# Attention scores on 32-by-32 tiles of TensorE in place of 32-by-128 ones

## The chip, the cores and the metric

The kernel runs on one core of one Trainium2 chip. The metric is the device time of one execution in microseconds (us). Before the change it is 2890.68 us, the median of three runs (2889.41 to 2895.76).

## The reference, cut to what matters

The input x is an image of 256 x 256 positions with 128 channels, float32. Two layers follow each other, each added to its input. The change touches only the first, an attention along rows: every one of the 256 rows `s` is an attention of its own, with 256 queries, 256 keys, 4 heads and 32 channels per head.

```python
q = split_heads(jnp.einsum('...qi,oi->...qo', q_x, wq)) / np.sqrt(C_HIDDEN)
k = split_heads(jnp.einsum('...ki,oi->...ko', kv_x, wk))
v = split_heads(jnp.einsum('...ki,oi->...ko', kv_x, wv))
a = jnp.einsum('bshqd,bshkd->bshqk', q, k)
a = a + bias1 + bias2
a = jax.nn.softmax(a, axis=-1)
o = jnp.einsum('bshqk,bshkd->bshqd', a, v)
...
o = o * g
...
return jnp.einsum('...qi,oi->...qo', o, wo) + bo
```

`q_x` is x after a group normalisation, `kv_x` an input of its own, `g` a sigmoid gate. The line that the change rewrites is the fifth, `a = einsum(q, k)`: for each row and head a 256 x 256 matrix from 32 channels. The second layer (spectral convolutions, a small attention over tokens and several normalisations) is computed by other functions and isn't touched.

## The kernel before, in words

The function `layer0` reads x once for the group statistics, turns the weights and the bias, and then calls `Rows.run`, which does the 256 attention rows. After that `layer1` does the second layer; in the profile the rows take from about 100 to about 1650 us of the span.

`Rows.run` is a software pipeline written out by hand: inside `manual_schedule` the order of the calls is the order of the instructions on TensorE (PE), ScalarE (ACT), VectorE (DVE) and GpSimd (POOL). Iteration `i` emits, in this order: `scores(i)`, `project(i + 1)`, `turn(i + 2)`, `weigh(i)`, `out(i - 3)`, `spectrum(i - 4)`, `attend(i - 1)`. On PE a row is therefore a chain of bursts:

- `scores` (L272): scores, transposed, keys on partitions. For each half `c` of 128 keys and each head `h`, one matmul takes 32 partitions of `qkT` (the head's channels) as contraction, 128 keys as the stationary columns, 256 queries as the moving ones. So it uses a 32 x 128 tile of the PE array. The four heads lie on partitions 0-31, 32-63, 64-95 and 96-127, so four such tiles stand under each other in the array. Each head writes to a PSUM bank of its own: `sc[0]` holds heads 0 and 1, `sc[1]` heads 2 and 3, each bank 2 x 256 float32 (both halves `c`).
- `project` (L246, L247, L252, L256): queries and keys, values and gate of the next row, 128 x 128 tiles.
- `turn` (L235, L236): transposes of the row after next.
- `out` (L333) and `spectrum` (L346, L348): the output projection, transposes and a small transform of earlier rows.
- `attend` (L311, L316): weighted sums and sums of the weights of the row before, on 128 x 32 tiles, four column quarters side by side.

The other engines: ScalarE computes exponentials of the scores in four pieces (`exp`, L281), two of them in place in PSUM, and evicts `qkT` (L249), gate (L260), `xnT` and `kvT` (L238, L240) and the transform (L352). VectorE multiplies heads 0 and 1 by the exponential of the bias (L294), scales the attended values (L322, L323, L324), adds (L337) and takes statistics (L351). GpSimd multiplies heads 2 and 3 (L299), adds the two key halves (L303) and adds the output bias (L327). The score tiles have one buffer each (`bufs=1`), so `scores(i + 1)` must wait until L294 and L281 have read those of row `i`; the other PSUM tiles of the rows share four buffers.

Everything is float32. In the records of the profile, each float32 matmul stands as two weight loads (PEld, LDWEIGHTS) and two MATMUL passes on PE; a transpose stands as one of each.

For comparison there is one more place in the kernel that uses 32 x 32 tiles: the helper `skip` in `layer1` (L1215), which runs, for four output tiles `ps[j]` and four row quarters `i`, a matmul from row quarter `i` to column quarter `i ^ j`. In the tile `ups<-y` of the second half of the channels it comes in two parts of 16 matmuls with 256 moving columns each.

```python
for j in range(4):
    for i in range(4):
        r, o = slice(32 * i, 32 * i + 32), slice(32 * (i ^ j), 32 * (i ^ j) + 32)
        w = blk[r, r] if len(blk.shape) == 2 else blk[r, j]
        nc.tensor.matmul(rows_of(ps[j][o, :])[:, n], w, part[r, j], start=(k == 0), stop=stop)
```

## Time and profile before

| what | value |
|---|---|
| median time of three runs | 2890.68 us |
| span of the profiled execution | 2888.9 us |
| PE busy | 2651.2 us, 92% of the span |
| PE weight loads busy | 1941.7 us, 67% |
| DVE busy | 2008.1 us, 70% |
| POOL busy | 1679.9 us, 58% |
| ACT busy | 1491.0 us, 52% |
| granted TensorE clock, mean | 0.952 of full |
| score matmuls (L272): records, mean pass | 4096, 400 ns |
| score loads (L272): records, mean | 4096, 184 ns |

How to read it: a group of the page is a line of the kernel with its engine, operation, tiles and shapes; then busy time, mean duration of one, and, after the bar, the idle time of that engine just before it with what ended most of it. "32*128 32x256" of a matmul is the tile of the array (contraction rows * stationary columns) and the moving operand (partitions x columns). A view by stretches gives the busy time of each engine between two times, with the number of instructions in brackets; the order of time lists start, duration, engine, line and operation, with equal neighbours merged ("x16"). The duration of a merged line reaches to the modelled end of its last instruction, so the distance between starts says more about pace than the duration does.

### The profile page before, as it was taken

To read this page: it belongs to the slowest core of one execution; us is meant where nothing else is said; L and a number is where in the kernel's file an instruction comes from. 1 tells how busy PE (TensorE), PEld (TensorE's weight loads), DVE (VectorE), ACT (ScalarE), POOL (GpSimd) and SP (SyncE) were. 2 spreads that over 40 slices of the span, in tenths; PEclk is the share of its full clock that TensorE was granted. 3 is DMA by queue.
4 is the path that set the end of the run, shared out by engine and by line. 5 is a ranking of instruction groups with operands and counts; after the bars stand their busy time and mean duration, and the time that the engine had idled before them with its cause. 6 is when DMAs were issued, how large, how long until landed. Compare 5 with 4: busy or idle time off the path is not lost. (4 is left out here: it accounts for less than half of the span.)

```text
span 2888.9 us, 71477 instructions
## 1 busy us (share of the span) xinstructions
PE 2651.2 (92%) x29116; PEld 1941.7 (67%) x29116; DVE 2008.1 (70%) x3263; ACT 1491.0 (52%) x2849; POOL 1679.9 (58%) x1308
## 2 busy tenths in 40 slices
PE   6799999999999999999999899999889988799654
PEld 6677777777777777777777656778665555455532
DVE  7788888888888888888888744756645545365555
ACT  0477777777777777777777622200004611365132
POOL 0399999999999999999999800200114833111211
PEclk9999999999999999999999989999989989799865
DMA  9422222222222222222222101188879984798599
GB/s 369 164 67 67 67 67 67 67 67 67 67 68 69 68 67 69 68 66 71 67 67 67 41 19 53 34 278 271 277 236 319 310 296 137 251 360 305 187 359 337
DMA packets 246705, 430.12 MB, mean 149 GB/s; under 512 B 26278, under 2 KB 174201, under 8 KB 239976
## 3 DMA queue, kind: packets, MB, share of 16 engines
q1 hardware_dynamic: 206568, 335.34, 34.8%
q0 software_dynamic: 22912, 81.80, 7.4%
q10 hardware_dynamic: 16896, 8.39, 1.0%
q8 instruction: 231, 3.78, 0.5%
q14 instruction: 98, 0.80, 0.1%
HBM read 290.17 MB, written 135.27 MB: 147 GB/s over the span
## 5 line engine op out<-in xcount | busy, mean ns | idle before, releaser
L299 POOL TENSOR_TENSOR e<-e,b1T 128x1024 f32<-128x1024 f32 x256 | 606.0, 2367 | 165.3 <-PE u L348 90.4
L303 POOL TENSOR_TENSOR es<-e 128x512 f32<-128x512 f32 x512 | 639.4, 1270 | 20.1
L281 ACT ACTIVATE sc<-sc,b2T 128x512 f32<-128x512 f32 x512 | 339.0, 662 | 364.7 <-PE sc L272 356.4
L323 DVE RECIPROCAL av<-av 128x256 f32<-128x256 f32 x256 | 452.3, 1767 | 27.2 <-DVE og L322 1.4
L281 ACT ACTIVATE e<-sc,b2T 128x512 f32<-128x512 f32 x512 | 348.7, 681 | 0.0
L294 DVE TENSOR_TENSOR e<-sc,b1T 128x1024 f32<-128x1024 f32 x256 | 311.1, 1215 | 0.0
L272 PE MATMUL sc<-qkT 32*128 32x256 f32 x4096 | 293.5, 400 | 1.3 <-DVE e L294 1.3
L311 PE MATMUL av<-e,v 128*32 128x256 f32 x4096 | 274.7, 385 | 0.5 <-POOL e L299 0.5
L1332 PE MATMUL yps<-xt,mpT 128*128 128x256 f32 x1024 | 247.7, 396 | 17.8 <-DVE yt L1342 9.3
L272 PEld LDWEIGHTS sc<-qkT 32*128 32x128 f32 x4096 | 185.2, 184 | 112.3 <-issue 97.8
L322 DVE SCALAR_TENSOR_TENSOR og<-gate,av 128x256 f32<-128x256 f32 x256 | 107.7, 421 | 190.6 <-PE av L316 190.6
L1332 PEld LDWEIGHTS yps<-xt,mpT 128*128 128x128 f32 x1024 | 195.9, 196 | 56.8 <-DVE yt L1342 14.7
L1346 POOL DMA_DIRECT2D yd<-yt x32 | 17.8, 555 | 346.1 <-DVE yt L1342 346.1
L327 POOL TENSOR_TENSOR x<-xt,bo 128x256 f32<-128x256 f32 x256 | 187.5, 733 | 0.0
L246 PE MATMUL qk<-xnT,wT_wq 128*128 128x256 f32 x512 | 179.5, 432 | 1.7 <-ACT xnT L238 1.7
L252 PEld LDWEIGHTS gv<-wT_wv,kvT 128*128 128x128 f32 x1024 | 155.0, 192 | 13.4
L316 PE MATMUL av<-es,ones 128*32 128x256 f32 x2048 | 157.5, 379 | 2.6 <-POOL es L303 2.5
L333 PE MATMUL wo<-wT_wo,og 128*128 128x128 f32 x1024 | 156.8, 276 | 2.7 <-DVE og L324 2.7
L311 PEld LDWEIGHTS av<-e,v 128*32 128x32 f32 x4096 | 106.9, 109 | 76.1 <-POOL e L299 1.0
L348 PE MATMUL u<-adft,x 128*128 128x129 f32 x1024 | 156.4, 275 | 0.0
L252 PE MATMUL gv<-wT_wv,kvT 128*128 128x128 f32 x1024 | 156.0, 275 | 0.0
L1699 ACT ACTIVATE blocks<-h2ps,col 128x512 f32<-128x512 f32 x128 | 89.0, 776 | 129.5 <-PE h2ps L1200 129.5
(546 smaller groups left out, 5294.4 us busy)
## 6 DMA issues: line engine op xcount, KB each, us to landing
xt<-x1d SPq DMA_DIRECT2D x128, 512.0 KB
xb<-in_x_dram SPq DMA_DIRECT2D x32, 1024.0 KB
xt<-in_x_dram SPq DMA_DIRECT2D x128, 256.0 KB
kt<-in_L_conv_kv_x_dram SPq DMA_DIRECT2D x128, 256.0 KB
x1d<-x SPq DMA_DIRECT2D x256, 128.0 KB
y<-yd SPq DMA_DIRECT2D x62, 512.0 KB
gs<-Gd SPq DMA_DIRECT2D x384, 64.0 KB
yd<-yt POOLq DMA_DIRECT2D x32, 512.0 KB, 6.0
```

Source lines behind the costliest of these rows:

```text
L246: nc.tensor.matmul(ps[:, 0:256], wT["wq"], xnT, start=True, stop=True)
L252: nc.tensor.matmul(ps[:, 256 + c * P : 256 + (c + 1) * P], kvT[:, c * P : (c + 1) * P], wT["wv"], start=True, stop=True,)
L272: nc.tensor.matmul(sc[h // 2][:, h % 2, c * 256 : (c + 1) * 256], qkT[p, 256 + c * P : 256 + (c + 1) * P], qkT[p, 0:256], start=True, stop ...
L281: nc.scalar.activation(r["e"][1][:, :, c, :] if hp else z, z, AF.Exp, bias=b2T[:, c, s : s + 1])
L294: nc.vector.tensor_tensor(r["e"][0].rearrange("p h c q -> p (h c q)"), r.pop("sc").rearrange("p h x -> p (h x)"), b1T[:, 0:2].rearrange("p ...
L299: nc.gpsimd.tensor_tensor(e1, e1, b1T[:, 2:4].rearrange("p h c q -> p (h c q)"), ALU.mult)
L303: nc.gpsimd.tensor_tensor(r["es"][hp], e[:, :, 0, :], e[:, :, 1, :], ALU.add)
L311: nc.tensor.matmul(ps[hd, 0:256], r["v"][:, c, hd], r["e"][h // 2][:, h % 2, c, :], start=(c == 0), stop=(c == 1),)
L316: nc.tensor.matmul(ps[32 * h : 32 * h + 32, 256:512], self.ones, r["es"][h // 2][:, h % 2, :], start=True, stop=True,)
L323: nc.vector.reciprocal(rd, rd)
L327: nc.gpsimd.tensor_tensor(r["x1"], r["x"], bc(self.bo, 1, 2), ALU.add)
L1332: nc.tensor.matmul(rows_of(ps[j]), mpT[:, sc, tt], by_turn(xt[:, sc])[:, j], start=(sc == 0), stop=False,)
```

## The change

Each score matmul of 32 channels by 128 keys is cut into four of 32 channels by 32 keys. `g` counts them; head `h` in round `g` takes the 32 keys of the column quarter `(h + g) % 4`, so that in one round the four heads stand in four different row quarters and four different column quarters of the array, on a diagonal. In four rounds each head has written all four partition quarters of its PSUM bank. The values computed are the same, and so are the output tiles, their readers and everything after. The idea is that the array can hold sixteen 32 x 32 tiles[...] each with a short weight load of 32 columns in place of 128.

The number of score matmuls goes from 8 to 32 a row. Nothing else is edited.

```diff
             for c in range(2):
-                for h in range(4):
-                    p = slice(32 * h, 32 * h + 32)
-                    nc.tensor.matmul(
-                        sc[h // 2][:, h % 2, c * 256 : (c + 1) * 256],
-                        qkT[p, 256 + c * P : 256 + (c + 1) * P], qkT[p, 0:256],
-                        start=True, stop=True,
-                    )
+                keys = qkT[:, 256 + c * P : 256 + (c + 1) * P]
+                for g in range(4):
+                    for h in range(4):
+                        p = slice(32 * h, 32 * h + 32)
+                        o = slice(32 * ((h + g) % 4), 32 * ((h + g) % 4) + 32)
+                        nc.tensor.matmul(
+                            sc[h // 2][o, h % 2, c * 256 : (c + 1) * 256], keys[p, o], qkT[p, 0:256],
+                            start=True, stop=True,
+                        )
```

## The prediction

> **What bounds the kernel now.** I read the page first: which engine is full, and whether its clock is.

> ```profile
> span 2888.9 us, 71477 instructions
> ...
> PE 2651.2 (92%) x29116; PEld 1941.7 (67%) x29116; DVE 2008.1 (70%) x3263; ACT 1491.0 (52%) x2849; POOL 1679.9 (58%) x1308
> ...
> PEclk9999999999999999999999989999989989799865
> ...
> L281 ACT ACTIVATE sc<-sc,b2T 128x512 f32<-128x512 f32 x512 | 339.0, 662 | 364.7 <-PE sc L272 356.4
> ...
> L272 PE MATMUL sc<-qkT 32*128 32x256 f32 x4096 | 293.5, 400 | 1.3 <-DVE e L294 1.3
> ...
> L272 PEld LDWEIGHTS sc<-qkT 32*128 32x128 f32 x4096 | 185.2, 184 | 112.3 <-issue 97.8
> ```

> The line that changes is L272, the costliest group on PE, and PE waits only 1.3 us for data before it in the whole kernel. ScalarE waits for PE, not the other way round. There are 2048 such matmuls and 4096 records: each float32 matmul stands as two passes, each with its own load. Next, the busy time by stretch, inside the attention rows:

> ```profile
> core 0: us, PE busy (x) PEld busy (x) DVE busy (x) ACT busy (x) POOL busy (x), PEclk, DMA share, GB/s
> ...
> 700.00:1000.00 300.00, 300.00 (x3202) 228.31 (x3202) 244.27 (x355) 224.09 (x451) 277.93 (x201) 1.00 0.21 68
> 1000.00:1300.00 300.00, 300.00 (x3202) 228.26 (x3201) 242.96 (x353) 224.01 (x451) 277.85 (x201) 1.00 0.21 66
> ```

> PE has no gap at full clock; GpSimd has 7% to spare. 3202 records in 300 us, at 64 a row, are 50 rows of 6.00 us. But a busy PE need not be streaming at its peak, and the ends of matmuls are modelled, so I read the starts of one row in order of time:

> ```profile
> 999.58 0.70 PE L246 MATMUL qk<-xnT,wT_wq 128*128 128x256 f32 x2
> 1000.12 0.59 PE L247 MATMUL qk<-kvT,wT_wk 128*128 128x256 f32 x2
> 1000.55 0.61 PE L252 MATMUL gv<-wT_wv,kvT 128*128 128x128 f32 x4
> ...
> 1004.50 1.15 PE L272 MATMUL sc<-qkT 32*128 32x256 f32 x16
> 1005.58 0.70 PE L246 MATMUL qk<-xnT,wT_wq 128*128 128x256 f32 x2
> ```

> From start to start, L247's two passes over 256 columns take 1000.55 - 1000.12 = 0.43 us, 0.215 a pass. The scores take 1005.58 - 1004.50 = 1.08 us. Their 16 records run four abreast (one head in each quarter of the array's rows, all 128 columns used): 4 x 0.215 = 0.86 us of streaming, and 0.22 for the change of tile shape and the first load. So a row is a sum of PE bursts, and the change is worth what it does to this 1.08, times 256.

> [...]scores' first matmul starts 0.31 us after the last one of the sums (L316), where passes are otherwise 0.215 apart.[...] The 16 matmuls of one key half, at two loads and two passes, are 64.

> **The change, part by part.** It takes out 8 matmuls a row on 32x128 tiles (16 loads, 16 passes) and puts in 32 on 32x32 tiles (64 and 64), in the same place on PE; nothing moves elsewhere.

> Streaming: 64 passes, at best 16 abreast, are again 4 x 0.215 = 0.86 us. Nothing is gained: the array was full. First load: shorter, but with sixteen tiles to start it goes again. In the trace tiles start 6.7 ns apart: 15 x 6.7 = 0.10 us, against about 0.10 by which the 128-column first round was longer than a pass. Zero, within 0.02.

> Supply of instructions: new, and the only large term. The kernel has this burst already: L1215 in the second layer runs 32 float32 matmuls of 256 columns on 32x32 tiles, the row quarters turning through the column quarters as here. In order of time, PE:

> ```profile
> 2533.78 1.49 PE L1215 MATMUL ups<-y,bl 32*32 32x256 f32 x64
> 2535.20 1.80 PE L1200 MATMUL ups<-k_bsyn,gs 32*128 32x128 f32 x32
> ...
> 2544.69 1.49 PE L1215 MATMUL ups<-y,bl 32*32 32x256 f32 x64
> 2546.11 1.15 PE L1200 MATMUL ups<-k_bsyn,gs 32*128 32x128 f32 x29
> ```

> Start to start 1.42 us, twice the same, at full clock, and it too ends in a change of shape. Where do 1.42 - 1.08 = 0.34 us go? The loads of one such burst, in three short stretches of the order of time:

> ```profile
> 2523.30 0.25 PEld L1215 LDWEIGHTS ups<-y,bl 32*32 32x32 f32 x32 [0.84 <-ACT blocks L1699]
> ...
> 2523.76 0.10 PEld L1215 LDWEIGHTS ups<-y,bl 32*32 32x32 f32 x1
> ...
> 2523.95 0.36 PEld L1215 LDWEIGHTS ups<-y,bl 32*32 32x32 f32 x30
> ```

> 32 loads (16 matmuls) start in the first 0.15 us. Then two more (at 2523.54 and 2523.76), and the other 30 only from 2523.95, 0.65 after the burst began, as if the next instructions enter only when the first matmul's second pass is done. From there the matmuls come about 16.6 ns apart (15 in 0.25 us), not 6.7. So the second half starts late and is spread out. The burst in the changed kernel has two such halves (c = 0, 1).

> Sum: 256 x 0.34 = 87 us, and 0.345 by the third decimal of the starts gives 88. All of it lies on PE, which has nothing to hide it behind. 2890.7 + 88 = 2979 us.

> The rest at nothing: ScalarE's exponentials (L281) wait for the end of the scores; they start 0.34 later in a row 0.34 longer. Queued behind them on ScalarE are the qkT copy, gate, xnT and kvT, for which PE waits a row later: ScalarE has 1.44 us idle in each row, GpSimd 0.44, and both gain. DVE's multiply (L294) and the waits of the first scores on it keep their distance. The 24576 added loads and passes, 96 a row, must be fetched; a DMA share of 0.21 in these rows hides that. Layer 1 is untouched.

> **Rivals.**
> 1. The stall is that of L1215's input tiles (its second half reads another tile, with a DMA wait of its own)[...]. Then scores cost 4 x 0.215 + 0.22 as before: 2891, no change. Against: that tile's first load is in before the gap, so the wait was met, and the gap comes behind it.
> 2. Faster. Short loads let sixteen tiles start closer than 6.7 ns, so that the first round of 128-column loads is saved: 0.05 us a row, 2877. Against: in the bursts I read, whatever the tile shape, neighbouring tiles start 6.7 ns apart and no closer.
> 3. Slower than forecast. In bursts on 32x32 tiles that follow PE work without a gap, as the scores do, the last tiles come 42 ns apart (L1215 sps, loads at 2520.53, .57, .61). If the second half of the scores comes so, it takes 14 x (42.3 - 16.6) = 0.36 more: 0.70 a row, 3070. For: the same predecessor. Against: in none of the 256-column bursts does the second half do so.
> 4. Tiles of one head, which share rows and a PSUM bank, run one after another: 4 x 0.86 = 3.4 us instead of 0.86, 3550. Against: L1215 runs four tiles of one row quarter at once, and the weighted sums (L311) four in one bank.

> **How the numbers follow.** Forecast 0.68, with 2960 to 3000 around it: the burst's leftovers from the sums before it may shift the halves by some 0.05. No change 0.08, faster 0.05, the 42 ns pace in whole or part 0.16, one after another 0.03. The range runs from 2945 (some 60% of the stall) to 3068 (nearly all of rival 3), which leaves out rivals 1, 2 and 4. Faster by over 0.2% 0.05, within 0.2% 0.08, slower 0.87.

> **What would show it.** Right: scores as 16384 records on 32*32 tiles; start to start of scores to the next L246 about 1.42 us; rows of 6.34; a hole of some 0.2 us in the loads after 32 to 34 of 64; ScalarE's wait for scores near 1.4 a row or more; other PE rows unchanged. Wrong: if scores still take 1.08 (rival 1), if loads of the second half stand 42 ns apart (3), or if passes of one head are 0.215 apart (4); and if PE gets waits on ScalarE or DVE, my zero for those was wrong.

## The result and the profile after

The changed kernel takes 2976.48 us, the median of four runs (2975.59 to 2983.31), against 2891.12 us (2889.41 to 2895.76, the three runs above and one more) before. The ratio is 1.0293 with a 95% interval of 1.0278 to 1.0308: 85 us slower. The forecast was 2979.

The lines of the page of the kernel after, with the same groups as before (line numbers in the changed kernel are two or three higher):

```profile
span 2981.5 us, 96053 instructions
...
PE 2740.0 (92%) x41404; PEld 1963.0 (66%) x41404; DVE 2004.5 (67%) x3263; ACT 1497.4 (50%) x2849; POOL 1680.1 (56%) x1308
...
PEclk9999999999999999999999989999999989799965
...
L283 ACT ACTIVATE sc<-sc,b2T 128x512 f32<-128x512 f32 x512 | 339.0, 662 | 445.8 <-PE sc L275 437.5
...
L275 PE MATMUL sc<-qkT 32*32 32x256 f32 x16384 | 383.0, 385 | 1.3 <-DVE e L296 1.3
...
L275 PEld LDWEIGHTS sc<-qkT 32*32 32x32 f32 x16384 | 210.1, 103 | 156.3 <-issue 97.3
```

The score matmuls now stand as 16384 passes on 32*32 tiles, with loads of 103 ns each in place of 184, and PE is 89 us longer busy, nearly all of it in this line (383.0 against 293.5). DVE, ACT and POOL are busy as long as before. PE has the same 1.3 us of waiting for data before the scores; ScalarE waits 81 us longer for them. So TensorE waits for nothing new: the burst itself got longer, and the other engines wait longer for it. By stretches, inside the rows:

```profile
core 0: us, PE busy (x) PEld busy (x) DVE busy (x) ACT busy (x) POOL busy (x), PEclk, DMA share, GB/s
...
700.00:1000.00 300.00, 300.00 (x5300) 220.29 (x5273) 231.15 (x335) 212.88 (x425) 262.76 (x191) 1.00 0.21 65
1000.00:1300.00 300.00, 300.00 (x5280) 220.65 (x5280) 229.47 (x334) 213.35 (x428) 262.70 (x190) 1.00 0.20 63
```

PE is as full as before (300.00 of 300 us) at the same granted clock of 1.00, and the load of the other engines has thinned by 5%, as a row got 6% longer. The order of time on PE, start, duration, line, count:

```profile
1003.02 0.61 PE L318 MATMUL av<-es,ones 128*32 128x256 f32 x8
1003.57 1.50 PE L275 MATMUL sc<-qkT 32*32 32x256 f32 x64
1004.99 0.70 PE L246 MATMUL qk<-xnT,wT_wq 128*128 128x256 f32 x2
1005.53 0.59 PE L247 MATMUL qk<-kvT,wT_wk 128*128 128x256 f32 x2
1005.96 0.61 PE L252 MATMUL gv<-wT_wv,kvT 128*128 128x128 f32 x4
```

From start to start the scores take 1004.99 - 1003.57 = 1.42 us where they took 1.08; every other burst has its old length (L247 again 0.43). The loads of that burst, in stretches of the order of time:

```profile
1003.56 0.35 PEld L275 LDWEIGHTS sc<-qkT 32*32 32x32 f32 x33 [0.41 <-issue]
...
1004.02 0.10 PEld L275 LDWEIGHTS sc<-qkT 32*32 32x32 f32 x1
...
1004.21 0.37 PEld L275 LDWEIGHTS sc<-qkT 32*32 32x32 f32 x30
```

34 loads, the last at 1004.02, then none until 1004.21: the hole that the second layer's burst showed before, at the same place.

By the records a row is 6.347 us long (median), against 5.997: 256 x 0.350 = 90 us. The last score pass of the last row starts at 1728.0 us of the span, before at 1640.8: 87 us later. The profiled execution of the changed kernel was the longest of its four (2983.31), and the rest of its distance to the one before lies behind the rows.

### The profile page after: what moved, and what is told of

Same layout as the page of the kernel before. It is cut to its first block, busy times and chain, and to the rows that moved or that the text cites. A ratio compares the mean times of both kernels' runs of the same rounds, so it can differ in the third digit from the quotient of the medians.

```text
span 2981.5 us, 96053 instructions
## 1 busy us (share of the span) xinstructions
PE 2740.0 (92%) x41404; PEld 1963.0 (66%) x41404; DVE 2004.5 (67%) x3263; ACT 1497.4 (50%) x2849; POOL 1680.1 (56%) x1308
## 5 line engine op out<-in xcount | busy, mean ns | idle before, releaser
L283 ACT ACTIVATE sc<-sc,b2T 128x512 f32<-128x512 f32 x512 | 339.0, 662 | 445.8 <-PE sc L275 437.5
L275 PE MATMUL sc<-qkT 32*32 32x256 f32 x16384 | 383.0, 385 | 1.3 <-DVE e L296 1.3
L275 PEld LDWEIGHTS sc<-qkT 32*32 32x32 f32 x16384 | 210.1, 103 | 156.3 <-issue 97.3
L258 DVE COPY v<-gv 128x256 f32<-128x256 f32 x256 | 108.6, 424 | 156.3 <-PE gv L256 156.3
L246 PE MATMUL qk<-xnT,wT_wq 128*128 128x256 f32 x512 | 179.5, 432 | 1.7 <-ACT xnT L238 1.7
L252 PEld LDWEIGHTS gv<-wT_wv,kvT 128*128 128x128 f32 x1024 | 155.0, 192 | 13.4
L252 PE MATMUL gv<-wT_wv,kvT 128*128 128x128 f32 x1024 | 156.0, 275 | 0.0
```

The source lines that it names most:

```text
L246: nc.tensor.matmul(ps[:, 0:256], wT["wq"], xnT, start=True, stop=True)
L252: nc.tensor.matmul(ps[:, 256 + c * P : 256 + (c + 1) * P], kvT[:, c * P : (c + 1) * P], wT["wv"], start=True, stop=True,)
L275: nc.tensor.matmul(sc[h // 2][o, h % 2, c * 256 : (c + 1) * 256], keys[p, o], qkT[p, 0:256], start=True, stop=True,)
L283: nc.scalar.activation(r["e"][1][:, :, c, :] if hp else z, z, AF.Exp, bias=b2T[:, c, s : s + 1])
```

## The experiments

Where the hole stands can be counted. By the records of the changed kernel, 34 loads and 33 passes have started ahead of it in each of the 256 bursts. Numbered in program order (load, pass, load, pass for each float32 matmul), the last of them is number 67. The next load starts 0.647 us into the burst (median), just after number 4, the second pass of the first matmul, has ended (modelled at 0.616). From number 4 to number 67 are 64. The tile of the eighteenth matmul stands empty meanwhile, by an estimate: the pass before on it starts at 0.248 and takes 0.216, so it is free at 0.464, yet no pass of the burst starts between 0.457 and 0.652, 0.19 us later.

### Tiles of 64 keys

```diff
-                for g in range(4):
+                for g in range(2):
                     for h in range(4):
-                        o = slice(32 * ((h + g) % 4), 32 * ((h + g) % 4) + 32)
+                        o = slice(64 * ((h + g) % 2), 64 * ((h + g) % 2) + 64)
```

> Scores on 32 x 64 tiles, two groups of 64 keys a head in place of four of 32: 16 score matmuls a row, 64 loads and passes together. Theory[...]: 64 fit, so no hole in the loads; scores take 1.05 to 1.09 us from start to start of the next burst, a row 5.97 to 6.01, the time 2884 to 2894 us. Rival (every additional small matmul costs its share, 0.35 us over 24 of them = 14.6 ns each): 8 more than before, 1.19 us, a row 6.12, about 2921 us.

Measured: 2892.32 us, against 2892.55 of the kernel before on the same chip; ratio 0.9998 (0.9985 to 1.0012). PE in order of time, and the loads of one burst:

```profile
1004.45 1.12 PE L275 MATMUL sc<-qkT 32*64 32x256 f32 x32
1005.50 0.70 PE L246 MATMUL qk<-xnT,wT_wq 128*128 128x256 f32 x2
```

```profile
1004.45 0.67 PEld L275 LDWEIGHTS sc<-qkT 32*64 32x64 f32 x32 [0.41 <-issue]
1005.49 0.19 PEld L246 LDWEIGHTS qk<-xnT,wT_wq 128*128 128x128 f32 x1 [0.38 <-issue]
```

Scores take 1.05 us, in the range of the theory; the rival's 1.19 is out. Twice the matmuls of the kernel before cost nothing. By the records the burst is even 0.027 us shorter than before (1.049 against 1.076 from start to start): with first loads of 64 columns, not 128, the second passes begin 0.267 us into the burst, before 0.320, and the four more tiles that each round has to start take 0.027 of this back (4 x 6.7 ns, an estimate). But the row is only 0.007 shorter (5.990), which a later run takes up.

### The same 32 matmuls in another order

```diff
-            for c in range(2):
-                keys = qkT[:, 256 + c * P : 256 + (c + 1) * P]
-                for g in range(4):
+            for g in range(4):
+                for c in range(2):
+                    keys = qkT[:, 256 + c * P : 256 + (c + 1) * P]
                     for h in range(4):
```

> The changed kernel's 32 matmuls in another order: for each group g first the key half c = 0, then c = 1, which stands on the same four tiles. Instructions, tiles and work are the same. Theory[...]: the 64 that fit now lie on 8 tiles, not 16, two matmuls behind each other on each, and what comes next waits for the oldest: 8 abreast, 64 passes / 8 x 0.215 = 1.72 us and more with the waits, scores about 2.1 us start to start, a row 7.0, about 3150 us. Rival (cost by the number of small matmuls): 1.42 as in the changed kernel, 2976 us. Second rival[...]: 16 abreast all the same, 1.42 or less.

Measured: 3167.59 us in one run. PE in order of time, then the loads of this burst in stretches:

```profile
1002.14 2.22 PE L275 MATMUL sc<-qkT 32*32 32x256 f32 x64
1004.29 0.70 PE L246 MATMUL qk<-xnT,wT_wq 128*128 128x256 f32 x2
```

```profile
1002.14 0.64 PEld L275 LDWEIGHTS sc<-qkT 32*32 32x32 f32 x34 [0.41 <-issue]
...
1002.78 0.17 PEld L275 LDWEIGHTS sc<-qkT 32*32 32x32 f32 x7
...
1003.00 0.10 PEld L275 LDWEIGHTS sc<-qkT 32*32 32x32 f32 x1
...
1003.21 0.66 PEld L275 LDWEIGHTS sc<-qkT 32*32 32x32 f32 x22
```

The scores take 2.15 us (the theory expected about 2.1), with the same instructions on the same tiles. Both rivals said 1.42 or less and fall. The loads show how: 34 start ahead of the first hole here too, 17 matmuls, though the first sixteen now lie on 8 tiles, not on 16. Then 8 more, four matmuls' worth, seven of them when the first four in order are done, and the next only at 1003.21. By then the ninth to twelfth matmul have finished, yet no load starts between 1003.00 and 1003.21, while older ones still run. (By the records their second passes start 0.30 us after the burst began, those of the fifth to eighth at 0.67; a record does not name its matmul, so this goes by the order, the free tiles and the 0.216 us of a pass.) That is what "in program order" means in this burst.

Counted one by one, the reach was 64 in this burst too. Number the instructions of this burst load, pass, load, pass. Numbers 65 and 66 are the first load and pass of the seventeenth matmul, on a tile that nothing has used yet. By the records the load starts 0.157 us into the burst, while number 2, the first pass of all, is still under way; the pass starts only at 0.425, once number 2 is done (its modelled end is 0.398). So with number 2 as the oldest that is not done, 65 has started and 66 has not. Likewise 69, a load on another free tile, starts at 0.645, after number 4 is done (0.614), and 85 at 1.077, after number 20 (1.046).

### One pass in place of two

```diff
-            r["qkT"] = wk.tile([P, 512], FP, tag="qkT", name=f"qkT_{s}")
+            r["qkT"] = wk.tile([P, 512], mybir.dt.bfloat16, tag="qkT", name=f"qkT_{s}")
```

This edit was made to the kernel before (e4 in the expectations) and to the changed kernel (e5).

> The kernel before with qkT in bfloat16, so that scores are computed with rounded queries and keys: one load and one pass per score matmul in place of two. It is the base for e5. 8 matmuls, 16 instructions a row; scores burst shorter by about 0.6 us than 1.08; then GpSimd at 5.6 us a row may set the pace. Both theories: about 2790 us, and the burst is to be compared with e5.

> The changed kernel with qkT in bfloat16 (rounded queries and keys): 32 matmuls on 32 x 32 tiles, but with one load and one pass each, 64 instructions a row. Theory[...]: they fit, no hole in the loads; first to last start of the burst within 0.06 us of e4's. Rival (14.6 ns for each additional small matmul): 0.35 us longer than e4's; rival by instructions (7.3 ns for each load-and-pass pair): 0.17 longer.

Measured: 2830.67 us for the first, 2832.85 for the second, one run each. The score bursts in the order of time, of the 32 x 128 tiles and then of the 32 x 32 tiles:

```profile
973.70 0.40 PE L272 MATMUL sc<-qkT 32*128 32x256 bf16 x8
974.03 0.70 PE L246 MATMUL qk<-xnT,wT_wq 128*128 128x256 f32 x2
```

```profile
973.91 0.44 PE L275 MATMUL sc<-qkT 32*32 32x256 bf16 x32
974.28 0.70 PE L246 MATMUL qk<-xnT,wT_wq 128*128 128x256 f32 x2
```

0.37 us against 0.33; by the records 0.170 against 0.130 from the first pass to the last, 0.040 longer, which is what twelve more tiles need at the 3.3 ns between starts in this burst (an estimate). The rivals asked for 0.35 or 0.17 more. So here 32 matmuls on 32 x 32 tiles cost 0.04 us: with one load and one pass each they are 64 instructions, and the hole is gone. This also tells instructions from matmuls: all 32 matmuls start here without a hole, where 17 did in float32. The kernels' times tell less, as PE is no longer the bound (busy 286 and 288 of 300 us between 700 and 1000 us, GpSimd 290 in both). The expected 2790 was too low: rows took 5.75 us, not GpSimd's 5.6; what sets the 5.75 was not looked for.

### The halves apart

```diff
             for c in range(2):
+                if c and s + 2 < NS:
+                    turn(s + 2)
                 keys = qkT[:, 256 + c * P : 256 + (c + 1) * P]
...
-                if i + 2 < NS:
-                    turn(i + 2)
```

> The changed kernel's 32 x 32 tiles, with the transposes of turn(i + 2) on PE between the two key halves, so that each half of 16 matmuls (64 instructions) is a burst of its own. Theory[...]: each burst has 0.36 us from first to last start and no hole, 0.66 us from start to the start of what follows; two further changes of tile shape cost about 0.2 us, so a row takes about 6.44 us and the kernel about 3000 us: 0.34 us saved on the hole and more than that spent on the shapes (0.10 net in the wrong direction). Rival (a cost of the number of small matmuls, wherever they stand): the 0.35 us stay, 0.53 us first to last start in each burst, a row of 6.8 us, about 3090 us.

Measured: 2994.09 us in one run. PE in order of time, and the loads of the first half:

```profile
1005.11 0.73 PE L277 MATMUL sc<-qkT 32*32 32x256 f32 x32
1005.77 0.33 PE L235 MATMUL tr<-ident,xt 128*128 128x128 f32 x1
...
1006.36 0.71 PE L277 MATMUL sc<-qkT 32*32 32x256 f32 x32
1007.00 0.70 PE L246 MATMUL qk<-xnT,wT_wq 128*128 128x256 f32 x2
```

```profile
1005.11 0.25 PEld L277 LDWEIGHTS sc<-qkT 32*32 32x32 f32 x32 [0.41 <-DVE stats L355]
```

All 32 loads of a half start without a hole, a burst is 0.36 and 0.34 us from first to last start by the records, and 0.66 and 0.64 to what follows. Two bursts with two additional changes of tile shape cost less score time (1.30) than one burst of both halves (1.42). The transposes between them grew from 0.44 to 0.59 (1005.77 to 1006.36), so the row is 0.03 us longer in sum, where 0.10 was expected. The edit also puts the two evictions of `turn` on ScalarE ahead of the exponentials; TensorE stays full all the same (300.00 of 300 us between 700 and 1000 us). Of the 11 us between this run and the profiled one of the changed kernel (2983.31), the rows account for about 7. The rival's 3090 is out.

### Where the 64-key version's gain went, and a version that keeps it

In the 64-key version (e1 in the expectations) the two transposes of `spectrum` took 0.238 us from their start to the next burst, before the change 0.218 (by the records; to two decimals it is 0.23 and 0.22). First the 64-key version, then before:

```profile
1008.23 0.40 PE L348 MATMUL u<-ident,x 128*128 128x128 f32 x2
1008.46 0.61 PE L350 MATMUL u<-adft,x 128*128 128x129 f32 x4
```

```profile
1008.31 0.38 PE L346 MATMUL u<-ident,x 128*128 128x128 f32 x2
1008.53 0.61 PE L348 MATMUL u<-adft,x 128*128 128x129 f32 x4
```

They write a PSUM buffer that ScalarE frees with the eviction of qkT (L249), which ends at 3.689 us after the start of the scores in the 64-key version and 3.677 before, while PE comes to the transposes 0.027 earlier. So the eviction was moved forward, past one exponential (the edit against the 64-key version; the control has the same move in the kernel before):

```diff
             nc.scalar.copy(r["qkT"], ps)
+            if s > 0:
+                rows[s - 1]["exp"](1, 0)
...
             exp(0, 0)
             exp(0, 1)
-            exp(1, 0)
...
+                    rows[i]["exp"](1, 0)
                     rows[i].pop("exp")(1, 1)
```

> The scores on 32 x 64 tiles of e1, and one exponential moved on ScalarE: that of heads 2 and 3, key half 0, comes after the eviction of the next row's qkT, not before it. In e1 the scores burst was 0.027 us shorter than before, but the row only 0.007, because the transposes of spectrum waited 0.020 us for their PSUM buffer, which ScalarE frees with the qkT eviction. If that is so, this eviction comes 0.57 us earlier, the wait goes, and a row takes 5.97 us: about 2885 us, 0.998 of before. If the wait is for something else, the row stays at 5.99 and the time at 2891.

> The kernel before with the same exponential moved, as the control for e6. Before, the transposes of spectrum do not wait, so both theories expect 2891 us, a ratio of 1.000, and a row of 6.00 us.

Measured: with 64-key tiles 2888.62 us against 2894.22 of the kernel before on the same chip, ratio 0.9983 (0.9970 to 0.9995); the control, the kernel before with the same move, 2892.34, ratio 0.9995 (0.9982 to 1.0007). PE of the first, in order of time:

```profile
1003.99 0.70 PE L246 MATMUL qk<-xnT,wT_wq 128*128 128x256 f32 x2
...
1006.72 0.38 PE L349 MATMUL u<-ident,x 128*128 128x128 f32 x2
1006.94 0.61 PE L351 MATMUL u<-adft,x 128*128 128x129 f32 x4
...
1009.96 0.70 PE L246 MATMUL qk<-xnT,wT_wq 128*128 128x256 f32 x2
```

The transposes are back at 0.218 us by the records (1006.72 to 1006.94), and a row is 1009.96 - 1003.99 = 5.97 us, as expected. So the 0.020 us were a wait for the eviction of qkT, and this is the fastest float32 version of the study, 0.17% under the kernel before (interval 0.05% to 0.30%). The control's row is 6.00 us by the records: the move alone gains nothing there, since before the transposes did not wait. The two intervals overlap, though, so it is the rows, not the times, that part the two versions.

## Why the prediction was right

- **PE sets the end of a row, and the scores count in full.** Right: PE stayed full at full clock, and 0.350 us a row times 256 is the 85 to 90 us measured.
- **No gain in streaming.** Right: before, the passes of the four heads already ran side by side on 32*128 tiles, in rounds 0.216 us apart. In the changed kernel sixteen 32 x 32 tiles do so: by the records their first passes start within 0.121 us, less than a pass takes (0.216). In the 64-key version and the bfloat16 pair, where a burst has 64 instructions or fewer, the tile shape as such was worth 0.03 to 0.04 us, in one direction or the other.
- **The burst of the second layer carries over.** Right to 0.01 us: 1.42 predicted, 1.42 measured, 34 loads before the hole in both. The term of 0.34 us measured 0.350 by the records (1.426 - 1.076 from start to start). The prediction's third decimals were a little off: the bursts of the second layer give 1.425 - 1.076 = 0.349, not 0.345. Its two parts are both there: of the 0.350, an estimate from the records gives 0.19 to the late start of the second half, 0.14 to its wider spacing (14 x (16.6 - 6.7) ns) and the rest to the last round. The predicted cause, that the next instructions enter as the first matmul's second pass is done, held in the changed kernel (0.647 us against 0.616) and in the order experiment (0.645 against 0.614), which adds that the oldest in order counts; in the other runs a burst stayed at 64 instructions or fewer and had no hole.
- **The rest at nothing.** Right: other PE bursts kept their length; no new wait on PE. The added instructions show in the profile's DMA queue of kind "instruction": a share of 1.0% between 1000 and 1300 us, before 0.6%.
- **Rival 1 (a wait of L1215's own input)** falls: the scores have no such wait and the hole is there. **Rival 2 (faster)** falls: the tiles of the changed kernel start 6.7 ns apart. **Rival 3 (42 ns apart)** did not come; in the second half the matmuls start 16.6 ns apart. Why some bursts of the second layer show 42 stays open. **Rival 4 (one head's tiles one after another)** falls: 1.42 us leaves no room for it.
- **What was mis-stated.** The prediction put the step at the 16 matmuls of a half, 64 instructions; in the trace 34 loads, those of 17 matmuls, start ahead of the hole. In the two bursts counted above, the 64 begin at the oldest instruction that is not done, so once the first load and the first pass are done (0.399 us in the changed kernel) they reach into the seventeenth matmul. It changes no number.

## What to carry to other kernels

Count loads and passes, not matmuls or tiles, when a matmul is cut into smaller tiles: a float32 matmul was four instructions, and in the bursts of 128 tiles fell free and stood empty (0.19 us for the one estimated above). A cut that stayed at 64 cost nothing (2892.32 us against 2892.55), one at 128 cost 0.35 us a burst, and a worse order inside that burst 0.73 more, so in such a burst put instructions that run on different tiles next to each other. A burst of the same shape elsewhere in the same trace, read from start to start, was a good price here: it gave 0.349 us where 0.350 was measured.

## What was not expected

- The order of the same 32 matmuls was worth 191 us (3167.59 in one run against 2976.48), more than twice what the change itself cost.
- In the order experiment passes started out of program order where their tile was free: the ninth to twelfth matmul started at 0.06 us, before the fifth to eighth (0.46 us), which waited for their tiles. The reach of 64 goes by program order in that burst, the starts within it do not.
- In the 64-key version ScalarE's first exponential starts 1.254 us after the scores begin, before 1.240, though the last pass starts 0.027 earlier. Together with the eviction behind it, this is what ate the gain. TensorE's signal, for which ScalarE waits, itself comes later (1.170 us after the scores begin, before 1.157); why it does was not tried and stays open.
- The wider spacing went by instructions too. In the changed kernel the first 14 matmuls of a burst start 6.7 ns apart, the later ones 16 to 17. In the bfloat16 version of the 32 x 32 tiles the first 28 loads start 3.3 ns apart, the last four 8.3. Both times the pace changed after 56 instructions (14 x 4 and 28 x 2), and the slower one was about 4.2 ns an instruction (an estimate, 16.6 / 4 and 8.3 / 2). What sets it was not tried.
